# When the next image's group-norm statistics are taken: a move by one chunk in the first layer of a four-layer kernel

## The chip, the cores and the metric

The kernel runs on one core of a Trainium2 chip. The metric is the device time of one execution in microseconds (us). The core has a matrix engine (TensorE, "PE" in the profile, its weight loads "PEld"), a vector engine (VectorE, "DVE"), an activation engine (ScalarE, "ACT"), a general engine (GpSimd, "POOL") and SyncE ("SP"), which here issues the transfers between the chip's main memory and the on-chip memory. Each engine runs its own instructions in program order, and they wait for each other by semaphores.

## The reference

The input is a batch of 8 images with 384 channels of 32 x 32 pixels. Four layers follow one another, each of the form x + f(gn(x)), where gn is a group norm over 32 groups of 12 channels, taken per image over all its pixels:

```python
def _gn(v, G=32, eps=1e-5):
    B_, C_, H_, W_ = v.shape
    g = v.reshape(B_, G, C_ // G, H_, W_)
    m = jnp.mean(g, axis=(2, 3, 4), keepdims=True)
    s = jnp.var(g, axis=(2, 3, 4), keepdims=True)
    return ((g - m) / jnp.sqrt(s + eps)).reshape(v.shape)

x = x + _L0_conv_ref(_gn(x), ...)   # a Mamba block over the 1024 pixels as a sequence
x = x + _L1_conv_ref(_gn(x), ...)   # 1x1, filter on 8x8 patches, 3x3 depthwise, gate, 1x1
x = x + _L2_conv_ref(_gn(x), ...)   # layer norm, Mamba block, MLP
x = x + _L3_conv_ref(_gn(x), ...)   # 3x3 depthwise convolution
```

The core of layers 0 and 2 is the selective scan. For each of 768 inner channels and 16 states it computes h[t] = exp(dt[t] A) h[t-1] + dt[t] u[t] B[t], then y[t] as the sum of h[t] C[t] over the states, along all 1024 pixels of an image.

## The kernel before

**Chunks and steps.** An image is cut into two chunks of 512 pixels (`NCH` = 2, `T` = 512). There are 32 chunks: 0 to 15 are layer 0 on images 0 to 7, and 16 to 31 are layer 2 on the same images. An even chunk is the first half of an image (`c` = 0), an odd one the second (`c` = 1). Layer 1 of an image runs beside the scan of the following chunks in the first sixteen, layer 3 likewise in the last sixteen. In main memory, `in_x` is the input and `x_mid` what layer 1 has produced.

A chunk has 24 steps (`NQ`), each with four scans of 128 rows and 512 pixels. For step t these things happen, each in a loop of its own over all 768 steps:

- `begins` (SP): a load of 1024 KB, `g<-dud`, that spreads dt·u over the 16 states into one of five buffers `g`; every fourth step also `dts<-dtd`.
- `times` (POOL): g = g · B, over 128 x 2048 elements, about 4.5 us.
- `decays` (PE) and `exps` (ACT): the four decays exp(dt·A) into the four `dA` tiles in PSUM.
- `scans` (DVE): four scans; two write into `g`, two into `dA`, and these two are then multiplied by C on DVE (`g<-dA,bc`).
- `carries` (ACT), in even chunks only: the last column of each scan is kept as the start for the odd chunk.
- `states` (POOL): the two scans in `g` are multiplied by C, 128 x 1024 elements, about 2.4 us. In an even chunk this comes after the carry has been read.
- `gathers` (PE): the sum over the states into `y`, after which the `g` buffer is free for another load.
- `gatings` (DVE), every fourth step: `u<-y,z`.

**Work beside the scan.** `front(n)` prepares a chunk: load `xf`, group norm, in-projection, short convolution, dt, and the small stores `dud` and `dtd` from which the steps load. `gates` computes z. `finish` does the out-projection and the residual (`x<-ps_out,x`), then starts `layer1` after every odd chunk. `layer1` begins with its own statistics (`st<-x`, six) and ends with a store to `x_mid`.

**The statistics.** `measure(s)` (line 480) loads one image in six pieces of 256 KB (`xk<-in_x` or `xk<-x_mid`) through two `xk` buffers, so a piece two places on can only be loaded once DVE has read the earlier one. For each piece `group_stats` (line 436) issues a `bn_stats` on DVE (`st<-xk`), then one aggregation (`mv<-st`), and then a short chain between PE and ACT (`ps_gn`, `gnm`, `gsp`, `grstd`, `gnb`) for the scale and bias. The normalisation of chunk n in `front(n)` needs the statistics of the image to be there.

**What sets the order.** The program is written out once, in an order found by a planner in the kernel itself. Every strand of work is a Python generator. The class `Order` holds all of them, with a table of when each engine is free and when data is known by its own cost figures (`Clocks`), and always continues the strand that could begin first. At equal times the loops of the scan go first on PE, ACT and SP; then on DVE and ACT the one that has been ready longest, and on the others the one that is due first. The instructions of each engine, SP's loads included, run in the order in which the planner issued them.

`start_jobs(t)` (line 1345) is called after the scans of each step; at the first step of a chunk it adds the strands for that chunk. In the kernel before, the strand `measured(m)` of an image is added at the start of the even chunk that lies two chunks ahead of the image's first chunk, in both layers. It has a due time, `t + NQ + 4`, that orders it only among strands which could begin at the same time. For layer 2, `measured` also waits until layer 1 of the same image is done. The first image's statistics are taken by `measure_first`, from the tiles that are loaded at the start.

Of the kernel before, what the change touches and what calls it, by code (L numbers as in the profile page):

```python
# [9 lines left out]
F32 = mybir.dt.float32  # L10
# [6 lines left out]
P = 128  # L17
B, C, H, W = 8, 384, 32, 32
# [8 lines left out]
NCH = L // T  # L27
# [12 lines left out]
NQ = ND * NSUB  # L40
# [14 lines left out]
def _flat(ap):  # L55
    return ap.rearrange("p a b -> p (a b)")
# [193 lines left out]
def tile_conv_preact_d4(ctx: ExitStack, tc: tile.TileContext, a: dict, out: bass.AP):  # L250
# [5 lines left out]
    wk = ctx.enter_context(tc.tile_pool(name="wk", bufs=1))  # L256
# [5 lines left out]
    order = Order(clocks)  # L262
# [6 lines left out]
    def mm(out_, lhsT, rhs, start=True, stop=True):  # L269
        tensor.matmul(out_, lhsT, rhs, start=start, stop=stop)  # L270
# [3 lines left out]
    def new(pool, shape, dtype, tag, bufs=1, name=None):  # L274

        t = pool.tile(shape, dtype, tag=tag, name=name or tag, bufs=bufs)
        ring = rings.setdefault((id(pool), tag), [])
        if len(ring) >= bufs:
            clocks.born[t.name] = clocks.last.get(ring[-bufs], 0.0)
        ring.append(t.name)  # L280
        return t

    def on(engine, *aps, when=None, due=None, next_=False):


        def ready():
            t = when() if when else 0.0
            return None if t is None else max(t, clocks.known(*aps) if aps else 0.0)

        return engine, ready, due, next_  # L290
# [5 lines left out]
    def once(test):  # L296
        return None, lambda: 0.0 if test() else None, None, False
# [21 lines left out]
    def ps_take(name):  # L319
        tag, t = min(banks, key=lambda x: x[1])  # L320
        banks.remove((tag, t))
        ps = psg.tile([P, 512], F32, tag=tag, name=name, bufs=1)
        clocks.born[ps.name] = t
        return ps, tag

    def ps_give(ps, tag):
        banks.append((tag, clocks.last[ps.name]))
# [46 lines left out]
    def act(out_, in_, func, **kw):  # L374
        if func in (AF.Exp, AF.Ln):
            if act_set["now"] != "exp":
                exp_set()
        elif func not in (AF.Identity, AF.Copy, AF.Square, AF.Abs):
            if act_set["now"] != func:
                clocks.free["ACT"] += 1.28  # L380
            act_set["now"] = func
        scalar.activation(out_, in_, func, **kw)

    def rsqrt(out_, in_, eps):
        act(out_, in_, AF.Ln, bias=eps)
        act(out_, out_, AF.Exp, scale=-0.5)
# [49 lines left out]
    def group_stats(blocks, read=None):  # L436
        st = new(wk, [P, 2 * KC, 6], F32, "st", 2)
        mv = new(wk, [P, 2], F32, "mv", 2)
        for h, k, v, then in blocks():
            yield on("DVE", v)  # L440
            vector.bn_stats(st[:, h * KC + k, :], v)
            if then:
                yield from then()
        if read:
            read()
        yield on("DVE", st)
        vector.bn_aggr(mv, _flat(st))
        nmean, spread, rstd, nbias = (
            new(wk, [P, 1], F32, tag, 4) for tag in ("gnm", "gsp", "grstd", "gnb")
        )  # L450
        yield on("PE", mv, when=bank)
        ps, tag = ps_take("ps_gn")
        mm(ps[:, 0:1], gmat, mv[:, 0:1])
        yield on("ACT", ps)
        act(nmean, ps[:, 0:1], AF.Copy, scale=-1.0)
        ps_give(ps, tag)
        act(spread, mv[:, 0:1], AF.Square, bias=nmean)
        act(spread, spread, AF.Identity, bias=mv[:, 1:2])
        yield on("PE", spread, when=bank)
        ps, tag = ps_take("ps_gn")  # L460
        mm(ps[:, 0:1], gmat, spread)
        yield on("ACT", ps)
        rsqrt(rstd, ps[:, 0:1], eps_gn)
        ps_give(ps, tag)
        act(nbias, nmean, AF.Identity, scale=rstd)
        return rstd, nbias
# [5 lines left out]
    def measure_first():  # L472
        def blocks():
            for h in range(NCH):
                for k in range(KC):
                    yield h, k, first[h][:, k, :], None

        chunks[0]["stats"] = yield from group_stats(blocks)

    def measure(s):  # L480
        yield on(None, when=xk_free.when)
        xk_free.take()

        def load(h, k):
            x = new(wk, [P, T], F32, "xk", 2)
            sync.dma_start(x, _rows(s["src"][s["b"], :, h * T : (h + 1) * T])[:, k, :])
            return x

        places = [(h, k) for h in range(2) for k in range(KC)]
        loaded = []  # L490
        for h, k in places[:2]:
            yield on("SP")
            loaded.append(load(h, k))

        def blocks():
            for q, (h, k) in enumerate(places):

                def then():
                    if q + 2 < len(places):
                        yield on("SP")  # L500
                        loaded.append(load(*places[q + 2]))

                yield h, k, loaded[q], then

        s["stats"] = yield from group_stats(blocks, xk_free.give)
# [69 lines left out]
    def gates(s, h):  # L575
        n = s["n"]
        yield once(lambda: "normed" in s and "loaded" in s["w"] and (n == 0 or chunks[n - 1]["gated"] >= (NH if h == 0 else ND)))
        z = s["z", h] = new(wk, [P, NH, T], F32, "z", 2)

        def block(d):  # L580
            ps, tag = yield from projection(s, "ps_z", "z", (h * NH + d) * P)
            yield on("ACT", ps)
            act(z[:, d, :], ps, AF.Copy)
            ps_give(ps, tag)

        yield from together(s["t"] + (6 if h else -4), [block(d) for d in range(NH)])
        yield on("ACT", z, when=session())
        act(_flat(z), _flat(z), AF.Silu)
        exp_set()
        s["gates", h] = True  # L590
# [242 lines left out]
    def scans():  # L833
        for t, (s, i) in enumerate(steps):
            for j in range(4):
                yield on("DVE", dAs[j], when=lambda: (
                    None if ("exp", t, j) not in said or ("times", t) not in said
                    else clocks.known(s["g", i][:, j, :])
                ))
                g = s["g", i]  # L840
                low = 4 - SHARE[i % NSUB]
                q = 4 * i + j
                vector.tensor_tensor_scan(
                    g[:, j, :] if j < low else dAs[j],
                    dAs[j],
                    g[:, j, :],
                    0.0 if s["c"] == 0 else carry[:, q : q + 1],
                    ALU.mult,
                    ALU.add,
                )  # L850
                ahead["scans"] += 1
                said["scan", t, j] = True
            for j in range(low, 4):
                yield on("DVE", dAs[j])
                vector.tensor_mul(g[:, j, :], dAs[j], s["bc"][:, 1, :])
                said["product", t, j] = True
            start_jobs(t + 1)
# [211 lines left out]
    def layer1(s):  # L1069
# [4 lines left out]
        def blocks():  # L1074
            for h in range(2):
                for k in range(KC):
                    yield h, k, x[h][:, k, :], None

        gn = yield from group_stats(blocks)
        hurry = s["n"] == B * NCH - 1  # L1080
        for hb in range(H // PS):
# [184 lines left out]
    def layer3(s):  # L1266
# [68 lines left out]
    chunks = [  # L1335
        {"pre": pre, "src": src, "b": b, "c": c, "n": (q * B + b) * NCH + c, "gated": 0}
        for q, (pre, src) in enumerate((("l0_", a["x"]), ("l2_", x_mid)))
        for b in range(B)
        for c in range(NCH)
    ]  # L1340
# [4 lines left out]
    def start_jobs(t):  # L1345
        n, i = divmod(t, NQ)
        if i or n >= len(chunks):
            return
        s = chunks[n]
        order.add(gates(s, 1), t + 8)  # L1350
        if s["c"] == 0 and n + NCH < len(chunks):
            m = chunks[n + NCH]
            order.add(measured(m), t + NQ + 4)
        if n + 1 < len(chunks):
            later = chunks[n + 1]
            order.add(front(later), t + NQ - 26)
            order.add(gates(later, 0), t + NQ - 4)
        order.add(finish(s), t + NQ + 10)

    def measured(s):  # L1360
        if s["n"] >= B * NCH:
            yield once(lambda: "done" in chunks[NCH * s["b"] + NCH - 1])
        yield from measure(s)
# [10 lines left out]
    def begun():  # L1374
        yield once(lambda: "fronted" in chunks[0])
        order.add(gates(chunks[0], 0), 1)
        start_jobs(0)
# [159 lines left out]
```

## Time and profile before

| | |
|---|---|
| median of 3 runs | 6210.31 us (6209.75 to 6211.98) |
| the profiled execution | 6204.07 us |
| its span, first to last instruction | 6202.2 us |
| mean granted TensorE clock | 0.973 |
| `bn_stats` on `xk` (measured images) | 90, 675 ns each |
| `bn_stats` on `x` (layers 1 and 3) | 96, 676 ns each |
| loads of `xk` | 42 from `in_x`, 48 from `x_mid` |
| POOL's multiplications `g<-g,bc` | 1536, 5243.4 us |

The profile is of one execution. It lists every instruction with its engine, start and duration, and, where an engine was idle before an instruction, what ended that idleness. Names such as `st<-xk` are the tile written and the tiles read. Nearly all instructions are recorded by one helper (line 189), so groups are told apart by their tiles and not by their lines. "PE g", "DVE g" and so on stand for an instruction of that engine which writes that tile; SPq is SyncE's queue of transfers.

### The profile page before, as it was taken

What the parts mean: (1) busy time and instruction counts of PE and PEld (TensorE: products, weight loads), DVE (VectorE), ACT (ScalarE), POOL (GpSimd) and SP (SyncE); (2) the same over time, 40 slices, a digit from 0 to 9 for tenths busy, and PEclk for the clock granted to TensorE, in tenths of its full rate; (3) what the DMA queues carried; (4) which work ended last, traced back from release to release, by engine and by line L of the source; (5) the groups of instructions that cost most, each with busy time, mean ns of one, the idle gap of its engine ahead of it and who ended that gap; (6) DMA issues with size and microseconds to landing.
All of it is one profiled execution on the core that took longest, in us unless ns stands there. A gap on an engine that the chain in (4) does not pass through costs nothing.

```text
span 6202.2 us, 62614 instructions
## 1 busy us (share of the span) xinstructions
PE 5799.2 (94%) x19022; PEld 2184.1 (35%) x19022; DVE 5616.8 (91%) x6381; ACT 4241.3 (68%) x7942; POOL 5725.3 (92%) x2028
## 2 busy tenths in 40 slices
PE   6878999999999999999989999999999999999998
PEld 2223333333333333333333333333333333333333
DVE  5999999999998999998887899899998999989994
ACT  5656677677667767776676676777767777677753
POOL 4999999999999999989997999999999999999991
PEclk8889999999999999999999999999999999999999
DMA  6877878877887888787777888878888788888871
GB/s 178 193 184 186 195 190 194 204 188 193 190 193 185 196 205 189 192 205 186 180 185 183 199 196 219 200 198 209 198 215 201 200 207 198 212 205 197 207 197 58
DMA packets 346724, 1195.88 MB, mean 193 GB/s; under 512 B 40516, under 2 KB 142580, under 8 KB 248084
## 3 DMA queue, kind: packets, MB, share of 16 engines
q1 hardware_dynamic: 346388, 1191.88, 79.1%
q8 instruction: 152, 2.49, 0.2%
q14 instruction: 184, 1.51, 0.1%
HBM read 1040.73 MB, written 150.99 MB: 192 GB/s over the span
## 4 chain that ended last, share of the span: by engine, by line
DVE 25%; PE 13%; POOL 8%; DMA 4%; issue 4%; ACT 4%; SPq 0%; POOLq 0%; DVEq 0%; ACTq 0%
DVE g L189 11%; DVE dA L189 8%; POOL g L189 6%; DVE u L189 2%; PE ps_dn L189 2%; PE ps_up L189 2%; PE ps_dw L189 2%; PE y L189 2%; PE dA L189 2%; DMA g<-dud 2%; DVE ps_dw L189 1%; PE ps_z L189 1%; DMA dts<-dtd 1%; PE ps_out L189 1%; DVE st L189 1%
## 5 line engine op out<-in xcount | busy, mean ns | idle before, releaser
L189 POOL TENSOR_TENSOR g<-g,bc 128x1024 f32<-128x1024 f32 (+1 forms) x1536 | 5243.4, 3447 | 248.1 <-ACT carry L189 94.1
L189 ACT ACTIVATE dA<-dA,w_A 128x512 f32<-128x512 f32 x3072 | 2018.6, 661 | 931.0 <-PE dA L189 919.4
L189 PE MATMUL dA<-dts,selr 96*128 96x512 bf16 x3072 | 1190.0, 390 | 233.2 <-DVE g L189 207.6
L189 DVE TENSOR_TENSOR_SCAN g<-dA,carry,g 128x512 f32<-128x512 f32 x768 | 955.4, 1269 | 75.1 <-POOL g L189 61.1
L189 DVE TENSOR_TENSOR g<-dA,bc 128x512 f32<-128x512 f32 x1536 | 994.5, 677 | 17.3 <-ACT carry L189 16.4
L189 DVE TENSOR_TENSOR_SCAN g<-dA,g 128x512 f32<-128x512 f32 x768 | 909.4, 1209 | 85.7 <-POOL g L189 77.8
L189 DVE TENSOR_TENSOR_SCAN dA<-dA,carry,g 128x512 f32<-128x512 f32 x768 | 952.2, 1271 | 28.0 <-ACT dA L189 27.4
L189 DVE TENSOR_TENSOR_SCAN dA<-dA,g 128x512 f32<-128x512 f32 x768 | 909.0, 1212 | 62.3 <-ACT dA L189 61.7
L189 PE MATMUL y<-g,sely 128*32 128x512 f32 x6144 | 857.0, 627 | 38.0 <-POOL g L189 35.6
L189 PEld LDWEIGHTS <-selr 96*128 96x128 bf16 x3072 | 300.2, 98 | 1113.0 <-issue 1072.0
L189 PE MATMUL ps_in<-xf,w_in 128*128 128x512 f32 x1152 | 562.7, 610 | 10.0 <-ACT xf L189 7.6
L189 PE MATMUL ps_z<-xf,w_z 128*128 128x512 f32 x1152 | 567.8, 597 | 3.6 <-DVE dt L189 3.6
L189 PE MATMUL ps_up<-t,mw 128*128 128x512 f32 x1152 | 556.0, 596 | 7.1 <-DVE u L189 5.2
L189 PE MATMUL ps_out<-u,w_out 128*128 128x512 f32 x1152 | 547.5, 594 | 0.4 <-ACT carry L189 0.4
L189 PE MATMUL ps_dn<-h,mw 128*128 128x512 f32 x1152 | 545.3, 594 | 1.6 <-ACT h L189 1.6
L189 PE MATMUL ps_dw<-tp,diag 128*128 128x512 f32 x864 | 438.8, 609 | 9.6 <-ACT diag L189 9.6
L189 PEld LDWEIGHTS y<-g,sely 128*32 128x32 f32 x6144 | 126.3, 109 | 599.2 <-issue 313.0
L189 PEld LDWEIGHTS ps_in<-xf,w_in 128*128 128x128 f32 x1152 | 218.6, 195 | 263.8 <-issue 234.2
L189 POOL TENSOR_TENSOR dt<-dt,u 128x512 f32<-128x512 f32 x192 | 244.3, 1274 | 72.4 <-PE ps_dr L189 56.3
L189 PEld LDWEIGHTS ps_dn<-h,mw 128*128 128x128 f32 x1152 | 217.8, 190 | 259.9 <-issue 235.3
L189 PEld LDWEIGHTS ps_up<-t,mw 128*128 128x128 f32 x1152 | 214.4, 190 | 267.2 <-issue 230.4
L189 PEld LDWEIGHTS ps_z<-xf,w_z 128*128 128x128 f32 x1152 | 215.9, 191 | 252.7 <-issue 215.2
(118 smaller groups left out, 6451.1 us busy)
## 6 DMA issues: line engine op xcount, KB each, us to landing
g<-dud SPq DMA_DIRECT2D x768, 1024.0 KB, 8.2
dtd<-pc SPq DMA_DIRECT2D x192, 384.0 KB, 4.0
dts<-dtd SPq DMA_DIRECT2D x192, 384.0 KB, 7.8
mw<-in_l_mlp_w SPq DMA_DIRECT2D x192, 384.0 KB, 6.5
dud<-dt SPq DMA_DIRECT2D x768, 64.0 KB, 3.2
xf<-in_x SPq DMA_DIRECT2D x16, 768.0 KB, 9.1
x<-in_x SPq DMA_DIRECT2D x16, 768.0 KB, 11.9
x_mid<-x SPq DMA_DIRECT2D x16, 768.0 KB, 7.0
```

Of the source, the lines that this page charges most:

```text
L189: return call(out_, *args, **kw)
```

## The change

In `start_jobs`, the strand `measured` of an image in layer 0, and of the first image of layer 2, is added at the start of an odd chunk, three chunks ahead of the image's first chunk. It was added two chunks ahead, at the start of an even one. A mark, `asked`, keeps an image from being measured twice. Chunk 0 still adds the measurement of chunk 2, since there is no odd chunk before it. For the other images of layer 2 nothing is different: at `n + NCH < B * NCH` the new distance ends. The four one-column tiles that hold the results get six buffers in place of four, as more results are alive at once.

```diff
@@ group_stats
         nmean, spread, rstd, nbias = (
-            new(wk, [P, 1], F32, tag, 4) for tag in ("gnm", "gsp", "grstd", "gnb")
+            new(wk, [P, 1], F32, tag, 6) for tag in ("gnm", "gsp", "grstd", "gnb")
         )
@@ start_jobs
         order.add(gates(s, 1), t + 8)
-        if s["c"] == 0 and n + NCH < len(chunks):
-            m = chunks[n + NCH]
-            order.add(measured(m), t + NQ + 4)
+        ahead_by = NCH + 1 if s["c"] == 1 and n + NCH < B * NCH else NCH
+        for m in chunks[n + NCH : n + NCH + 2]:
+            if m["c"] == 0 and "asked" not in m and m["n"] - n <= ahead_by:
+                m["asked"] = True
+                order.add(measured(m), t + NQ + 4)
         if n + 1 < len(chunks):
             later = chunks[n + 1]
             order.add(front(later), t + NQ - 26)
```

## The prediction

> **What bounds the kernel now.** First the page, for the engines' shares and the chain that ended last:
>
> ```profile
> PE 5799.2 (94%) x19022; PEld 2184.1 (35%) x19022; DVE 5616.8 (91%) x6381; ACT 4241.3 (68%) x7942; POOL 5725.3 (92%) x2028
> DVE 25%; PE 13%; POOL 8%; DMA 4%; issue 4%; ACT 4%; SPq 0%; POOLq 0%; DVEq 0%; ACTq 0%
> ```
>
> PE, DVE and POOL are all above 90%, and the chain changes hands between them, so the average decides nothing. I therefore cut the span at the first scan of each chunk (there are 96 scans a chunk) and asked for the busy time of each stage. Columns: window, its length, then busy us of PE, PEld, DVE, ACT, POOL, then clock, DMA share, GB/s. These are chunks 8 (even: first half of an image), 9 (odd) and 10, then two cuts inside chunk 8:
>
> ```profile
> 1506.40:1696.00 189.60, 172.30 (x603) 65.45 (x602) 172.85 (x205) 136.80 (x297) 176.42 (x63) 0.96 0.79 190
> 1696.00:1865.30 169.30, 164.50 (x561) 61.78 (x558) 164.95 (x181) 116.51 (x211) 168.64 (x54) 1.00 0.82 196
> 1865.30:2057.90 192.60, 175.37 (x603) 66.55 (x602) 173.09 (x206) 136.94 (x297) 176.49 (x63) 0.95 0.79 189
> ...
> 1521.00:1562.00 41.00, 39.94 (x135) 14.61 (x136) 39.55 (x49) 31.05 (x65) 39.75 (x15) 1.00 0.72 185
> 1562.00:1584.00 22.00, 21.61 (x73) 8.25 (x72) 15.41 (x20) 10.57 (x22) 16.82 (x7) 1.00 1.00 247
> ```
>
> The odd chunk is bound by POOL (168.64 of 169.30), with DVE only 4.4 us short of it. The even chunk is 20 us longer and no engine fills it: POOL idles 13.2 us, DVE 16.8 us. The even chunk holds all twelve statistics, six of the measured image (in the first cut) and six of layer 1. What are POOL's waits, in the even and then in the odd chunk?
>
> ```profile
> POOL g L189 <- DMA g<-dud: 6.3, 3, 4.0
> POOL g L189 <- ACT carry L189: 5.2, 2, 2.9
> ...
> POOL g L189 <- DVE g L189: 0.5, 1, 0.5
> ```
>
> And where: POOL's order of time through the stretch with the measured statistics (the bracket is idle time before):
>
> ```profile
> 1540.18 6.83 POOL L189 TENSOR_TENSOR g<-g,bc 128x2048 f32<-128x2048 f32 x2 [0.73 <-DMA g<-dud]
> ...
> 1566.57 6.83 POOL L189 TENSOR_TENSOR g<-g,bc 128x1024 f32<-128x1024 f32 x2 [2.25 <-ACT carry L189]
> 1576.34 13.77 POOL L189 TENSOR_TENSOR g<-g,bc 128x1024 f32<-128x1024 f32 x4 [2.93 <-ACT carry L189]
> ```
>
> The stall begins when the measured statistics end (the last is at 1561.0). Before them POOL's second multiplication follows its scan by 9 to 11 us (steps 0 and 1 of the chunk, from the starts and ends of the instructions): DVE is ahead. At steps 7 and 8 it follows by 1.3 and 0.6 us: DVE has lost its lead, and POOL waits for scan and carry. Last, SyncE's queue, on which the six loads stand, and DVE's waits at steps 2 to 4 of the odd chunk:
>
> ```profile
> SPq L189 <- DVE st L189: 13.6, 4, 8.6
> ...
> DVE u L189 <- PE y L189: 1.3, 1, 1.3
> DVE g L189 <- POOL g L189: 0.5, 1, 0.5
> DVE dt L189 <- ACT spm L189: 0.3, 1, 0.3
> ```
>
> The loads have two buffers, so four of them wait on SP until a `bn_stats` has freed one, 13.6 us in all, up to 8.6 us at once, with the `g` loads queued behind.
>
> **What the Trainium skill says.** PSUM — Partial Sum Buffer, Engine vs sequencer instructions: the queues of ScalarE, VectorE and GpSimd are strict FIFO. The trace agrees: at 1583.65 DVE begins an `x<-ps_out` after 3.86 us of idleness with a scan queued behind it. DMA: Bandwidth & Descriptors, Issuing engines are not separate DMA queues: all issuers share the 16 engines, so moved loads compete wherever they go; the cut 1562 to 1584 shows it (share 1.00, 247 GB/s). SBUF — State Buffer, SBUF: two separate sides: DVE and GpSimd exclude each other only where DVE runs a 2-port mode or reads two SBUF inputs. `bn_stats` has one input and takes 675 ns for 512 columns, and POOL's wide multiplications take 4.5 us with or without it near; so I charge POOL no lock.
>
> **The change part by part.** Nothing is added or removed over the kernel. Seven measurements (first chunks of images 2 to 7 of layer 0, and of image 0 of layer 2) start at chunks 1, 3, ... 13 instead of 2, 4, ... 14; image 1 stays in chunk 0. The buffers 4 to 6 are four tiles of one column: no instruction, no time.
>
> One measurement is six `bn_stats` at 0.675 and one aggregation at 0.30 on DVE: 4.35 us. ACT: 0.17 + 3 x 0.295 + 0.26 + 0.20 = 1.5 us, into odd chunks where ACT idles 53 us: nothing. PE: four weight loads and four one-column matmul passes at about 0.2, some 1.7 us against 4.8 us of idle PE: nothing. DMA: 6 x 262 KB = 1.57 MB, at 247 GB/s 6.4 us, which lifts the odd chunk's share from 0.82 to 0.86: nothing by itself. SP: six issues at about 0.35, and the four waits.
>
> Gain in an even chunk. DVE gets 4.35 us back before step 7. POOL is full there, so it gains only its idle time: the wait of 2.25 us, less than the 4.35 by which the scan comes sooner, goes; the 0.73 for a `g` load held back on SP goes with the `xk` loads. The 2.93 I leave: that step's multiplication, scan, carry and second multiplication follow in series, POOL to DVE to ACT to POOL. Sum 2.98; bounds 0.73 (something else holds the scan) and 5.91 (all three). The next thing late is the out-projection (DVE idle 3.86), on a PE busy 21.61 of 22.00. Seven even chunks: -20.9.
>
> Cost in an odd chunk. 4.35 on DVE, less the 2.1 that it idles at steps 2 to 4 (1.3 + 0.5 + 0.3), less the 0.8 by which the second multiplication trails its scan where this is least afterwards (step 9): 1.4 us. Bounds 0 (the later slack of 4 us and more absorbs it) and, with nothing absorbed, 4.35. Behind DVE stand carries, POOL's second pass and PE's gathers. SP: a `g` load waits some 6 us landed before POOL takes it (steps 3 to 6), so of a hold of 8.6 us at most 2.6 would show; I take 0, as the hold shrinks when DVE takes the statistics promptly. Chunks 1 and 3: DVE idles 13.2 and 8.3 us, cost 0. Five chunks (5 to 13): +7.0.
>
> Sum: -13.9 against the profiled execution's own 6204.07 (span 6202.2 and 1.9 around it): 6190.2. The median of the runs, 6210.31, is 6.24 above that: 6196.4.
>
> **The rivals.** B, a better repeating order. The order is planned greedily, so an early shift moves everything behind it. Chunks 6 to 13 repeat one order, at 358.6 to 361.9 us a pair; chunks 4 and 5, with a slightly different order and the same kinds of work, took 354.6. For: this shows 4 us a pair in order alone. Against: it may as well go the other way. Five pairs x 4 = 20 us further: 6176.
>
> C, hidden anyway. PE is busy 39.94 of 41.00 and 21.61 of 22.00 through steps 2 to 9: if the backlog of out-projection and layer 1 sets these steps, the freed DVE time becomes waiting for PE; 0.73 x 7 = 5.1 stays and the odd chunk absorbs its part: 6205. Against: POOL's releaser at 1566.57 is a carry, not PE.
>
> D, slower: the odd chunk takes the full 4.35. DVE would stand at 164.95 + 4.35 = 169.30 of 169.30 beside POOL at 168.64, two full engines that feed each other over five `g` buffers; every wait that is left (y from PE, the gate) then lengthens the chunk. With the even chunk gaining only 0.73: 5 x 4.35 - 7 x 0.73 = +16.6: 6227. Against: POOL's second pass trails its scans by about 4 us and more from step 11 on. It decides from 4.2 us an odd chunk on at a gain of 2.98 (20.9 / 5), from 1.0 us at a gain of 0.73.
>
> **How the numbers follow.** A, the sum above, 0.55; its own range 6186 (half of the 2.93 goes too) to 6204 (half of the 2.25 stays). 0.2%, about what a measurement of this kernel tells from no change, is 12.4 us: faster is below 6197.9. Of A, 0.43 lie there and 0.12 between. B 0.14, faster. C 0.06, the same. D 0.25, slower: a chunk that is already full is a real objection. Faster 0.57, same 0.18, slower 0.25. The range runs from 6172, which leaves out the lower part of B, to 6229, which leaves out the upper part of D.
>
> **What would show it.** Right: no measured statistics in even chunks 2 to 14 and six in each odd chunk 1 to 13; even chunks at about 186 us with the carry wait after step 7 gone; odd chunks at 170 to 171, POOL still full. SP's wait for statistics moves to the odd chunks, without POOL waiting for `g` there. D: odd chunks at 173 or more, with POOL idle behind DVE scans or `g` loads. C: even chunks within 1 us of before, with DVE idle before `x<-ps_out` longer. B: pairs at 352 or less, with the steps of even chunks in another order. The forecast is wrong if the layer boundary (chunks 14 to 18: 197, 195, 185, 218, 193 us) moves by over 10 us, or the second layer's settled pairs (385 to 387) change: I have put both at nothing.

## The result: 44 us slower, and the loss is not where the change was made

The changed kernel takes 6253.74 us (median of 4 runs, 6250.21 to 6254.55) against 6210.03 us before: a ratio of 1.0069, 95% interval 1.0054 to 1.0084. That is outside the range that was forecast, and on the other side. The profiled execution of the changed kernel took 6253.29 us, its span is 6251.3 us.

The page of the changed kernel, the lines that answer to the two shown of before:

```profile
PE 5815.0 (93%) x19022; PEld 2203.6 (35%) x19022; DVE 5614.8 (90%) x6381; ACT 4243.1 (68%) x7942; POOL 5724.8 (92%) x2028
DVE 12%; PE 8%; POOL 7%; ACT 4%; issue 4%; DMA 1%; SPq 0%; DVEq 0%; POOLq 0%; ACTq 0%
```

The counts are the same, and the busy times differ by less than 20 us (PE 15.8 more, its weight loads 19.5): the same work in another order. The chain is again divided among the engines and decides nothing. The stage table of the changed kernel, cut as before at the first scan of each chunk (columns: window, length, busy us of PE, PEld, DVE, ACT, POOL, then clock, DMA share, GB/s), shows where it went. First an odd and an even chunk of the first layer (7 and 8), then chunks 25 and 26 of the second layer, then the last two:

```profile
1340.80:1518.60 177.80, 170.78 (x579) 64.54 (x576) 168.69 (x189) 127.28 (x226) 173.46 (x56) 0.99 0.82 197
1518.60:1696.30 177.70, 165.02 (x587) 64.45 (x586) 167.69 (x197) 127.67 (x280) 171.60 (x61) 0.96 0.81 194
4732.90:4929.10 196.20, 182.26 (x585) 67.78 (x584) 180.93 (x201) 134.33 (x214) 191.94 (x69) 0.97 0.82 197
4929.10:5157.70 228.60, 214.08 (x665) 82.76 (x664) 188.07 (x219) 147.23 (x280) 181.03 (x71) 0.98 0.71 176
5737.20:5920.60 183.40, 177.00 (x580) 66.56 (x579) 171.41 (x195) 134.34 (x259) 177.44 (x70) 0.99 0.84 204
5920.60:6251.30 330.70, 301.48 (x861) 120.11 (x859) 217.39 (x256) 144.82 (x242) 174.80 (x60) 0.96 0.50 126
```

and in the kernel before, chunk 26 and the last one, 31:

```profile
4928.60:5115.60 187.00, 182.86 (x599) 69.30 (x600) 175.09 (x202) 137.41 (x267) 182.93 (x71) 1.00 0.85 207
...
5884.60:6202.20 317.60, 292.79 (x844) 116.73 (x842) 217.55 (x256) 143.50 (x239) 175.06 (x61) 0.96 0.50 129
```

In the first layer the unequal pair, 169.3 odd and 189.6 even, has become an equal one, 177.8 and 177.7, and a pair is shorter by 2 to 5 us (chunks 6 to 13). In the second layer, in which no statistics were moved, chunk 26 takes 228.6 us in place of 187.0 and the last chunk 330.7 in place of 317.6.

The sums, each worked out from the starts of chunks in the profiled executions (the last column is the median of the timed runs; chunk 0 is left out, for a reason given at the end):

| kernel | chunks 1 to 15 | chunks 16 to 30 | chunk 31 | median us |
|---|---|---|---|---|
| before | 2716.6 | 2905.9 | 317.6 | 6210.03 |
| changed | 2698.5 | 2954.3 | 330.7 | 6253.74 |
| difference | -18.1 | +48.4 | +13.1 | +43.7 |

Of the +48.4, chunks 16 and 17 have 7.5 us, chunk 19 has 9.9, chunk 26 has 41.6, and the other eleven together are 10.6 us shorter than before.

### The profile page after: what moved, and what is told of

It reads as the page before. It is cut to its first block, busy times and chain, and to the rows that moved or that the text cites. A ratio compares the mean times of both kernels' runs of the same rounds, so it can differ in the third digit from the quotient of the medians.

```text
span 6251.3 us, 62704 instructions
## 1 busy us (share of the span) xinstructions
PE 5815.0 (93%) x19022; PEld 2203.6 (35%) x19022; DVE 5614.8 (90%) x6381; ACT 4243.1 (68%) x7942; POOL 5724.8 (92%) x2028
## 5 line engine op out<-in xcount | busy, mean ns | idle before, releaser
L189 PEld LDWEIGHTS ps_out<-u,w_out 128*128 128x128 f32 x1152 | 217.4, 190 | 253.3 <-issue 241.6
```

What stands on the lines that cost most here:

```text
L189: return call(out_, *args, **kw)
```

## The experiments

Three theories were to be told apart.

- T1: the statistics are not what costs. The planner goes on greedily from wherever it stands, so the move gives all later work another order. In the second layer PE is full (in chunk 26 of before 182.86 of 187.00 us), and its background work (out-projection, MLP, layer 3) has hardly any time to catch up. Where the order lets this work fall behind the scan, the scan has to wait for it later, or it is left over after the last scan.
- T2: the moved statistics cost time where they now stand, in odd chunks that were full already, through DVE and through SyncE's queue.
- T3: it is the one move that touches the second layer, the statistics of its own first image, which upsets the boundary of the layers.

**Relieving PE in the second layer (e1, e2).** Both kernels with half of the MLP's hidden channels left out:

```diff
-        for g in range(2):
+        for g in range(1):
             h1 = new(p2, [P, NFH, T], F32, "h1")
...
-            if g == 1:
+            if g == 0:
                 s["taken"] = True
```

(and the same range for its weights). Expected of the base, the kernel before without that half:

> The kernel before, with the second half of layer 2's MLP left out (hidden channels 768 to 1535: 18 up and 18 down matmuls a chunk; its output lacks that part). It is only the base for the next run. PE in the second layer falls from about 98% busy to clearly less; about 150 us shorter than the kernel before, some 6060 us, with odd and even chunks of layer 2 at about 183 to 190.

and of the changed kernel without it:

> The changed kernel with the same half of the MLP left out. T1 (the loss is layer 2's background on a full PE: out-projection, MLP and layer 3 fall behind the scan, which then has to wait for them; the first layer itself gained): with PE relieved there is nothing to fall behind, and the first layer's gain comes through to the end: 12 to 20 us below e1. T2 (the moved statistics cost time where they now stand, through DVE and SyncE's queue in the full odd chunks): the loss of some 40 us stays, or at least the run is not below e1.

Measured: e1 6117.53 us, e2 6107.81 us; against the same runs of before, ratios of 0.9852 (0.9838 to 0.9867) and 0.9835 (0.982 to 0.985). The base was shortened by 89 us and not by 150: that guess was wrong. e2 lies 9.7 us below e1 in the medians, on the side that T1 forecast, but short of its 12 to 20. The stage tables of e1 and then of e2, chunk 25 and the last chunk:

```profile
4714.00:4903.00 189.00, 169.55 (x531) 59.46 (x534) 179.51 (x200) 124.33 (x197) 186.34 (x67) 0.91 0.80 192
5848.80:6120.60 271.80, 221.53 (x643) 79.46 (x641) 207.72 (x240) 119.55 (x205) 174.59 (x60) 0.88 0.52 130
```

```profile
4699.40:4888.30 188.90, 169.59 (x531) 59.46 (x534) 179.43 (x199) 124.23 (x197) 186.25 (x67) 0.91 0.81 191
5834.20:6104.80 270.60, 221.50 (x643) 79.50 (x641) 207.73 (x240) 119.51 (x205) 174.60 (x60) 0.88 0.53 130
```

PE is down to 170 of 189 us, and POOL, at 186, is now the fullest engine, which would explain why only 89 us were saved. From chunk 21 on the two kernels run the same second layer, to 0.2 us a chunk; the last chunk differs by 1.2. The jam of chunk 26 (its 41.6 us) and the longer end are gone, and the changed kernel is the faster one, by 9.7 us in the medians and 15.8 in the spans of the two profiled executions. Their chunks 1 to 15 take 2699.1 against 2723.5 us; some 7 us of that difference are chance, as before took 2716.6 with the order of e1. T2 falls: the same seven statistics stand in the same odd chunks. What the change loses needs the second half of the MLP. That half is load on PE (24 us of chunk 25), and it is also a link between one chunk's out-projection and the next; these two runs don't tell the load from the link. Chunks 16 and 17 are 7.0 us longer in e2 than in e1, as they are in the changed kernel (7.5); this part doesn't go with the MLP.

**Fewer moves (e3, e8).** The condition is written as a set of images, given by their first chunks:

```diff
+        for m in chunks[n + NCH : n + NCH + 2]:
+            early = m["n"] in (4, 8, 10, 12, 14, 16)
+            if m["c"] == 0 and "asked" not in m and m["n"] - n <= (NCH + 1 if early else NCH):
+                m["asked"] = True
+                order.add(measured(m), t + NQ + 4)
```

This is e3, all but chunk 6's; e8 has (4, 6, 10, 16). The sets were chosen because the order written for them repeats in the second layer as that of before does. So they test whether the order sets the time, and not whether it could have been foreseen from the moves.

> The changed kernel, but the statistics of one image (the one whose first chunk is 6) are taken where they were, at the start of chunk 4; the six other moves stay. T1: the order of layer 2 is found anew from wherever the planner stands at its start, and here it falls into the order of the kernel before (even chunks about 187, odd about 198, a last chunk of about 318); with the first layer's gain of 15 to 20 us, 6190 to 6197. T2: six of the seven moved statistics are still there, so six sevenths of the loss: about 6247.

> The changed kernel with four of the seven moves: images with first chunks 4, 6, 10, and the first of layer 2 (16); those with first chunks 8, 12 and 14 stay. T1: layer 2 falls into the settled order again and keeps the first layer's gain: about 6195. T2: four sevenths of the loss, about 6235.

Measured: e3 6191.95 us, ratio 0.9975 (0.9964 to 0.9986); e8 6195.56 us, ratio 0.9984 (0.9977 to 0.9991). Both are faster than before, with six and four of the seven moves in place. Chunk 26 and the last chunk in e3:

```profile
4920.90:5108.80 187.90, 182.80 (x600) 69.22 (x600) 175.28 (x203) 137.63 (x267) 183.77 (x72) 1.00 0.85 209
5877.00:6193.40 316.40, 292.04 (x843) 116.50 (x841) 217.49 (x256) 143.37 (x239) 174.85 (x60) 0.96 0.51 130
```

This is the second layer of before. Its chunks 16 to 30 take 2909.4 us (before 2905.9), and chunks 1 to 15 keep the gain: 2699.3, as in the changed kernel. e3 is better than both kernels.

**The move that touches the second layer (e5, e6).** e5 is the set (4, 6, 8, 10, 12, 14), e6 is (16) alone.

> The changed kernel, but the statistics of layer 2's first image stay where they were, at the start of chunk 14; the six moves inside the first layer stay. T3 (the one move that touches the second layer upsets the boundary): layer 2 is as before and only the first layer's gain is left, about 6192. T1 (which order layer 2 falls into depends on where the planner stands at its start, not on this move): it may fall into either kind; in the unsettled kind, with a last chunk of about 330 us and background work 20 us and more late, it is slower than before in spite of the gain, 6215 to 6255.

> The kernel before with only the statistics of layer 2's first image moved, from chunk 14 to chunk 13. T3: the loss of some 40 us is here. T1: chunks 0 to 12 as before, a different order at the boundary, and layer 2 either settled (even about 187, odd about 198, last 318: within 15 us of before) or not (30 us and more slower).

Measured: e5 6223.17 us, ratio 1.0024 (1.0013 to 1.0035); e6 6220.81 us, ratio 1.0021 (1.0014 to 1.0028). T3 falls in both: without that move the second layer still has the long kind (a chunk of 215.9, a last one of 329.7), and with that move alone it has the settled kind (187.0 and 198.3, last 317.6). What e6 loses (14 us in the medians) is seen only in part: chunks 16 to 30 of its profile are 8.5 us longer, with chunk 16 alone at 199.3 us for 185.3, but the profiled execution, 6211.40 us, was the fastest of its 20.

**One move alone, and no move at all (e4, e7).** e4 moves chunk 8's statistics only, the set (8). e7 leaves all statistics in their chunks; those of chunk 4 begin one step later:

```diff
+        if i == 1 and n < B * NCH - 1 and chunks[n]["c"] == 0 and n == 2:
+            order.add(measured(chunks[n + NCH]), t - 1 + NQ + 4)
         if i or n >= len(chunks):
             return
...
-        if s["c"] == 0 and n + NCH < len(chunks):
+        if s["c"] == 0 and n + NCH < len(chunks) and not (n < B * NCH - 1 and n == 2):
```

> The kernel before with the statistics of a single image moved (the one whose first chunk is 8: taken in chunk 5 and not 6). T1: one move is enough to break the repeating order; chunks 6 to 12 fall into unlike, mostly longer ones (the sixth or the tenth chunk near 190 to 205), layer 2 keeps none of the settled order of before, and the run is 30 to 60 us slower than before. T2: one seventh of the loss, 6 us, so 6216; everything behind chunk 7 as before.

> The kernel before with the statistics of one image (first chunk 4) begun one step later in the same even chunk (at step 1 of chunk 2 and not at step 0, some 7 us); nothing changes its chunk. T1: that is enough to lead the planner into another order from chunk 4 on: the unsettled kind in layer 2 (last chunk about 330 us) and 40 to 60 us more than before. T2 (it is the place in the full odd chunk that costs): no more than 5 us from before.

Measured: e4 6296.25 us, ratio 1.014 (1.0125 to 1.0155); e7 6288.09 us, ratio 1.0133 (1.0118 to 1.0148). One move costs twice what seven cost, and a delay of one step, with nothing moved to another chunk, costs nearly as much: 81 us. The stage table of e7, chunks 8, 9 and the last:

```profile
1515.80:1709.90 194.10, 181.61 (x618) 71.62 (x618) 171.50 (x201) 134.66 (x303) 174.01 (x61) 0.96 0.78 184
1709.90:1904.70 194.80, 186.96 (x617) 71.02 (x617) 171.77 (x193) 131.51 (x236) 174.72 (x57) 0.98 0.73 176
5962.10:6288.40 326.30, 300.17 (x863) 120.03 (x861) 217.23 (x257) 145.12 (x241) 174.48 (x60) 0.97 0.50 128
```

Here the first layer has lost its order too: chunks 1 to 15 are 30 us longer than before in e7 and 37 in e4, chunks 16 to 30 46 and 43 us, the last chunk 9 in both. The size was underrated in both (e4: 30 to 60 forecast, 89 measured; e7: 40 to 60 forecast, 81 measured); the first layer's 37 and 30 us are about what was missed.

**The same first layer, two second layers (e9, e10).** The kernel before, with the statistics of layer 2's first image begun one step (e9) or two steps (e10) into chunk 14, and not at its start. This is e9; e10 has 2 in both places:

```diff
+        if n == B * NCH - NCH and i == 1:
+            order.add(measured(chunks[B * NCH]), t - 1 + NQ + 4)
...
+            early = m["n"] in ()
+            if m["c"] == 0 and m["n"] != B * NCH and "asked" not in m and m["n"] - n <= (NCH + 1 if early else NCH):
```

> The kernel before; only the statistics of layer 2's first image begin one step later, at step 1 of chunk 14. The first layer's order up to chunk 14 is that of before. T1: layer 2 in the settled order (even about 187, odd about 198, last 318); the boundary somewhat shorter: 6195 to 6205.

> As the run before, but two steps later, at step 2 of chunk 14. T1: the same first layer again and some 7 us between the two starts, but layer 2 in the unsettled order (odd chunks here and there 205 to 216, last about 330): 20 to 45 us slower than the run before. T2, and any account by what the statistics cost where they stand: no difference between the two beyond 3 us.

Measured: e9 6200.62 us, ratio 0.9988 (0.9982 to 0.9995); e10 6239.57 us, ratio 1.0052 (1.0037 to 1.0067). The six loads begin 2.4 and 12.2 us after the first scan of chunk 14, and the kernels are 39 us apart, as forecast. Chunk 25 and the last chunk of e9, then of e10:

```profile
4728.80:4927.10 198.30, 193.53 (x622) 73.16 (x622) 188.35 (x214) 137.99 (x221) 186.87 (x68) 1.00 0.83 202
5882.40:6199.50 317.10, 292.22 (x843) 116.64 (x841) 217.43 (x256) 143.37 (x239) 174.80 (x60) 0.96 0.52 130
```

```profile
4736.10:4950.20 214.10, 206.42 (x641) 78.80 (x640) 189.61 (x215) 140.08 (x225) 193.41 (x71) 0.99 0.79 196
5904.20:6237.40 333.20, 306.17 (x867) 122.06 (x865) 218.20 (x258) 146.03 (x243) 175.71 (x62) 0.96 0.51 128
```

Up to chunk 14 the two have one order. So a loss in the second layer comes about without any change in the first, by 10 us in the start of six small loads.

**One order, one time.** The traces let the orders themselves be compared, instruction by instruction, on DVE, ACT and POOL. From the start of chunk 20 to the end, in one profiled execution of each:

| kernels with one and the same order | us from chunk 20 to the end |
|---|---|
| before, e3, e6, e8, e9 | 2427.8 to 2432.0 |
| e5, e10 | 2463.3 and 2465.5 |
| e4, e7 | 2478.3 and 2481.7 |
| changed | 2478.7 |

Kernels that share an order take the same time to 4 us, wherever their statistics stood, and the orders lie up to 50 us apart. So this much of T1 is shown: the order sets the time. That a full PE is what makes an order bad is argued, since in e4 and e7 the first layer lost too. The table also settles a rival: the four one-column tiles have six buffers in all these kernels but before and e7, which have four. e9 has six, and up to chunk 14 its order on these engines is that of before.

## What happens in the jam

The background's delay can be read from the ends of its instructions. In the kernel before, the MLP of a chunk ends 416 to 422 us after that chunk's first scan, for all of chunks 18 to 28. In e3 it is the same, and in e6, e8 and e9 to 1 us. In the changed kernel it is 422 to 491 us, with the most at chunk 24, and in e4, e5, e7 and e10 it is 430 to 480. Two conditions of the kernel's program meet here. The MLP of a chunk must have done all its up-products (`ps_up`, copied to `h`) before the out-projection of the next chunk may overwrite the tiles `t`, and that out-projection must be done before `front`, two chunks on, may overwrite the tiles `u`. The order of time of ACT in chunk 26 of the changed kernel (start, duration; the normalised `xf` of chunk 27, the last `t` of chunk 25, the first `u` of chunk 27):

```profile
5018.14 2.23 ACT L189 ACTIVATE xf<-xf,vec 128x512 f32<-128x512 f32 x3 [0.87 <-DVE xf L189]
...
5051.08 0.59 ACT L189 ACTIVATE t<-ps_out 128x512 f32<-128x512 f32 x1
...
5058.55 0.78 ACT L189 ACTIVATE u<-ps_in,w_vec 128x512 f32<-128x512 f32 x1 [0.20 <-PE ps_in L189]
```

and in the kernel before, the same three:

```profile
5004.20 0.80 ACT L189 ACTIVATE xf<-xf,vec 128x512 f32<-128x512 f32 x1
...
5005.57 0.58 ACT L189 ACTIVATE t<-ps_out 128x512 f32<-128x512 f32 x1
...
5008.43 0.78 ACT L189 ACTIVATE u<-ps_in,w_vec 128x512 f32<-128x512 f32 x1 [0.87 <-PE ps_in L189]
```

Before, the MLP of chunk 24 writes its last `h` as chunk 26 begins; the normalisation ends at 5005.0 and the out-projection's copy at 5006.2, 78 us into the chunk, and the in-projection follows at once. Changed, that last `h` comes 63 us into chunk 26. `xf` is ready at 5020.4, but the out-projection of chunk 25 is done at 5051.7, 123 us into the chunk, and the in-projection starts after it. Everything that follows in `front(27)` is late by as much and more: its first dt is there 198 us after chunk 26's first scan, and not 132. In the kernel before the scan of chunk 27 begins at 187; here the last step of chunk 26 lasts 40.7 us.

At the end, DVE waits for the MLP's products, in the changed kernel and then in the kernel before:

```profile
DVE x L189 <- PE ps_dn L189: 79.5, 8, 35.4
```

```profile
DVE x L189 <- PE ps_dn L189: 69.3, 7, 30.5
```

This wait is 10.2 us longer, of the last chunk's 13.1: PE has more to do in that chunk (301.48 us busy for 292.79).

That the wait for the out-projection makes this jam is read from the trace and not tested by a run of its own: a kernel with a third pair of `u` tiles was not run. e1 and e2 show only that the jam needs the second half of the MLP. Which decision of the planner at the boundary leads to the one order or the other stays open; it is not one of the moves, as e3, e5 and e6 show. And chunks 25 of e10 and 26 of the changed kernel are different jams: in e10 DVE waits longest for POOL and a store.

## Why the prediction was wrong, step by step

- **The sum for the first layer** (-13.9): the sign is right, and that the size came near is luck. Chunks 1 to 15 measure -18.1, and -17.3 in e3, but the parts don't match. The forecast spreads its sum as -4.6 over chunks 1 to 5, -6.3 over chunks 6 to 13 and -3.0 over 14 and 15; measured are +8.9, -14.8 and -12.2. Chunks 1 and 3, put at 0, lost 4.1 and 3.2.
- **Its two terms**: both mis-sized. The even chunk gained 12.2 us (mean of chunks 6, 8, 10 and 12: 190.3 to 178.1) and not 2.98; the odd chunk lost 8.5 (169.3 to 177.8) and not 1.4. Of the wait for `g` loads in the even chunk, 6.3 us, only the 0.73 beside the statistics was priced. The other two waits stand over 50 us behind the last statistics; first POOL's order of time in chunk 8 of before, then its waits in chunk 8 of the changed kernel:

```profile
1617.74 6.85 POOL L189 TENSOR_TENSOR g<-g,bc 128x2048 f32<-128x2048 f32 x2 [4.04 <-DMA g<-dud]
1626.16 16.08 POOL L189 TENSOR_TENSOR g<-g,bc 128x2048 f32<-128x2048 f32 x5 [1.58 <-DMA g<-dud]
```

```profile
POOL g L189 <- ACT carry L189: 4.1, 4, 2.7
...
POOL g L189 <- DMA g<-dud: 0.2, 1, 0.2
```

So POOL's idle time in the even chunk fell from 13.2 to 6.1 us, nearly all of it this wait. The rest of the gain is work that POOL now does in the odd chunk: its busy time fell from 176.4 to 171.6 in the even one and rose from 168.6 to 173.5 in the odd one. More moved than the statistics: in the odd chunk ACT's busy time rose from 116.5 to 127.3 us and PE's from 164.5 to 170.8, and fell in the even one by 9 and 7. By tiles it is the `gate` of layer 1, a block of z with one evaluation `z<-z`, the table loads of ACT (10 before and 6 after in the even chunk, 6 and 10 in the odd), and one step's eight gathers. Rival D's price for the odd chunk (4.35) was too low as well, but D assumed an even chunk that gains almost nothing.
- **SyncE's queue, taken at 0**: nearly right in the odd chunk. The wait moved and grew, and POOL waits 0.8 us for `g` loads there. Every transfer of this kernel stands on this queue, so no run here shows issuers sharing the 16 DMA engines; the cut 1562 to 1584 (share 1.00) shows loads of one issuer that fill them. In chunk 7 of the changed kernel, of SyncE's waits and of POOL's:

```profile
SPq L189 <- DVE st L189: 19.5, 3, 8.8
```

```profile
POOL g L189 <- DVE g L189: 3.3, 4, 1.0
POOL g L189 <- DMA g<-dud: 0.8, 2, 0.6
```

- **"The carry wait after step 7 gone", "even chunks at about 186"**: POOL's waits for the carry are 4.1 us in chunk 8, for 5.2 before, and one of 2.69 us stands there still. It was not the one wait of 2.25 us that made the even chunk long.
- **"The next thing late is the out-projection (DVE idle 3.86)"**: most of this cost nothing. POOL's multiplication for the scan queued behind it ended at 1583.2 us, and the scan began at 1584.3, so it was held up by about 1 us.
- **The layer boundary put at nothing**: held within its 10 us. Chunks 14 to 18 take 981.9 us in place of 989.1.
- **The second layer's settled pairs put at nothing**: this is the step that failed, and alone turns the sign: +48.4 and +13.1 us. The prediction said itself, under B, that an early shift moves everything behind it and "may as well go the other way", and named a change of the settled pairs as a sign of being wrong; but it priced only a gain, in the first layer. It took the second layer's repeating order (385 to 387 us a pair) for a property of the work. The runs show two kinds of order for the same work, one that repeats (before, e3, e6, e8, e9: last chunk 316 to 318) and one that doesn't (changed, e4, e5, e7, e10: 326 to 333, with single chunks behind chunk 18 of 205 to 229), and that 10 us at one place can decide between them.
- **Rival D, the slower side** (0.25): the right sign for the wrong reason. Its own marks are there, odd chunks over 173 us with POOL waiting for DVE (3.3 us, above), but the first layer gained in spite of them, and e2 and e3, faster with these moves in place, exclude D as the cause of the loss.

## What to carry to other kernels

Where a greedy planner writes the order of a whole program, a change is not local: follow the new order to its end before costing the edit, and look above all at the stage with the fullest engine, however far behind the edit it lies. A background chain whose engine is nearly full (PE 98% busy in chunk 26 of before) has little room to catch up. Its distance behind the main loop, read at the same event in each round, told the settled orders from the others here, where PE's share of the span (94% and 93%) did not. And when a change loses, test a change of no meaning, such as one step's delay, before blaming its content: here that cost 81 us, and six of the seven moves, with the rest of the order in another phase, gained 15.

## What was not expected of the hardware

Chunk 0 has one order of instructions in all twelve kernels, yet it took 187.6 to 195.0 us in their profiled executions. It goes with the granted clock of TensorE in that stretch. Chunk 0 of before, then of the changed kernel:

```profile
74.40:262.10 187.70, 141.54 (x429) 42.79 (x428) 159.64 (x181) 112.80 (x228) 172.32 (x60) 0.80 0.85 200
75.50:267.80 192.30, 145.69 (x429) 43.98 (x428) 159.72 (x180) 112.56 (x228) 172.24 (x60) 0.78 0.83 195
```

DVE and POOL are busy for the same time in both, and PE takes 4.2 us more for the same 429 matmuls. In order of the clock: 0.81 in e2 and e9 (187.6 and 187.7 us), 0.80 in before, e4 and e10 (187.7 to 188.6), 0.79 in e1, e6, e7 and e8 (188.2 to 190.2), 0.78 in e5 and the changed kernel (190.7 and 192.3), 0.77 in e3 (195.0). Why the clock differs from one execution to another is not shown. This is why the sums above start at chunk 1: chunk 1 starts 5.7 us later in the changed kernel's profile than in that of before, and this is no part of the change.
